# A re-planned prologue: first keys copied out of PSUM without their bias, two left-over values on four column quarters, left-over keys and values behind the second head's queries

## The chip, the cores and the metric

The kernel runs on one core of a Trainium2 chip. Its time is the device time of one execution in microseconds (us), as a median of several executions. Work is spread over five engines with queues of their own: PE (TensorE) multiplies and writes into PSUM, DVE (VectorE) and ACT (ScalarE) read PSUM and SBUF, POOL (GpSimd) works in SBUF, and SP issues most of the transfers between HBM and SBUF. An engine works through its queue in order and waits at an instruction until the semaphores it names are there.

## The reference

```
x   = residual + mha(layernorm(x), layernorm(ctx))      # 4096 queries, 3202 keys, H=512, 8 heads of 64
U   = (layernorm(x) @ W_in.T + b_in) @ Bmat
s_t = silu(s_{t-1} @ A.T) + u_t                          # 64 states, over the 4096 rows
out = x + states @ Cmat + (mean(ctxb) @ W_prog.T + b_prog)
```

Here only the front of it matters: keys `k = ln(ctx) @ Wk.T + bk` and values `v = ln(ctx) @ Wv.T` of all 3202 rows (the bias of the values goes into the output's row), and the queries of the first 512 rows. Everything is float32.

## The kernel before, in words

**Stages.** A prologue (`lead`) makes all keys and values and writes them to HBM (`kd`, `vd`), prepares weights, and makes the first queries. Then the main part goes over 8 blocks of 512 queries and 4 pairs of heads, loading keys and values again as it goes; each step is a pair of score and output products. The last part ends the recurrence. Only the prologue's order differs between the two kernels.

**The prologue.** The 3202 rows are 26 chunks: 25 of 128 rows and one of 2 (`REST`). Four chunks make a group; `ct` holds a group's normalized rows turned (features on the partitions), two groups at a time. Groups 0 and 1 are turned on PE (`tp_c`) and copied out of PSUM by ACT or DVE (`copy_chunk`); groups 2 to 5 are flipped by DVE in blocks of 32 (`pair`, L639) and moved into place by sixteen transfers on SP (`ct<-pair`, L651). The transfers of a group are numbered by four parts `a`; the first two parts hold the group's first two chunks.

Keys and values of a group come from a seven-product scheme (`Seven`), names `"1"` to `"7"`, each product being four matmuls of 128x256 (`pkx`, `pky`, `pvx`, `pvy`: the k or v side, bank x or y). Sums of quarters of `ct` (`t`, by DVE, L950) and of the weights (`sk`, `sv`, by POOL, L923) are operands. Bank x takes products 1, 6, 7, 4 in turn, bank y 2, 5, 3. After product 1 alone, `keep` copies bank x out of PSUM (outcome `"11"`); only then may product 6 go on adding into that bank. On the keys' side `keep` is two activations that add the key bias on the way; that bias (`wk.bias`) needs a chain of its own: four DVE instructions of `shift_wk`, four thin PE matmuls (`pb`, L1024) and a DVE sum (L1031). `join` (pieces `tied`) then adds bank y to the kept tile by DVE; product 5 may go into bank y only after that. `keep` for the other outcomes (`"12"`, `"22"`, `"21"`) works the same way.

Chunks 0 to 3 make values by plain products (`whole_chunk`, `pv`, four matmuls of 128x512). So does the end of the prologue: chunk 24 and the two rows of chunk 25. For those two rows `whole_chunk` splits the four matmuls over two column halves of the array (`parts = 2`), and `last_values` adds the two halves, which lie on different partitions of PSUM, and sends them to `vx`. `keys_` makes the keys of the 130 rows left (`pk`, L884), a copy to `ks`, and a POOL copy of the last two keys to `kx` (`k.sample`). `heads` makes queries of a head pair half (`pq`, L398), and ACT copies them out as `q` (L408). The first scores against a sample of keys are `sm` (L436): they read `q` of the first two and `kx` of the first two.

**What sets the order.** `Plan.order` is a list scheduler that runs while the program is built: each piece has a cost, pieces it comes after, rings of buffers it takes and gives, and a due time; the due time is shifted by the table `SHIFT`, in units of `STEP` (2150). The earliest due piece that fits is taken. The result is one fixed order for each queue; nothing of the plan's own times is left at run time, only the order and the semaphores.

Of the kernel before, what the change touches and what calls it, by code (L numbers as in the profile page):

```python
# [14 lines left out]
ALU = mybir.AluOpType  # L15
# [4 lines left out]
T, S2, H, NH, HD, NS = 4096, 3202, 512, 8, 64, 64  # L20
P = 128
# [55 lines left out]
class Plan:  # L77
# [18 lines left out]
    SHIFT = {  # L96
        "a": 1.5, "add": 0.5, "add.h": 776.5, "add.l": -24.5, "added": 171.75, "b": 1, "base": 34.5, "c2": -4,
# [20 lines left out]
        "swap.h": 43.75, "swap.l": -4, "to": -50, "tq": 14.75, "weights": -83.5, "yb": 20.5, "a.load": -109.5,  # L118
        "bu": -32.25, "c.copy": 24, "c.factors": -82.75, "c.flip": -34.5, "c.load": -5.25, "c.move": -90,
        "c.scaled": 21.25, "c.stats": 504.75, "c.turn": -1, "d.bi": 113, "d.bm": -0.75, "d.cb": 32,  # L120
        "d.cb2": -19.25, "d.rows": 117.75, "d.win": 69.25, "d.wo": 105.5, "d.wq": 96.5, "d.x0": 34.75,
        "h0": 166, "h0.q": 30, "in": 539.5, "in.bi": 32, "in.bm": 6.75, "in.cb": 28.25, "in.cb2": -22.5,
        "in.rows": 190.25, "in.win": -29, "in.wk": 608.5, "in.wo": 72.5, "in.wq": -22.25, "in.x0": 10.5,
        "k": 57, "k.copy": -98, "k.sample": -40.75, "k.store": 39.75, "keep": -66.75, "marks": -168.25,
        "mean": -21.5, "modb": -40.75, "p": -663, "pb": 39.25, "pm": -330, "prm": -87.25, "prr": 28.25,
        "pt": -27.5, "pw": -174.25, "rowb": -43, "rowv": -84, "rowv.w": 39.75, "s": -19, "store": -169.25,
        "sums_": -3.25, "t": -142, "tied": -298.5, "v": 1.5, "v.copy": -50.25, "v.store": -78.25,
        "wcr": 33.75, "wct": -20.25, "wk": -206, "wk.bias": -112.5, "wk.g": -107.25, "wk.pb": -197.75,
        "wk.w": -368.5, "wq": -85, "wq.bias": -56.25, "wq.g": -303, "wq.pb": 70.5, "wq.w": -109.25,
        "wv": 73.75, "wv.bias": 25.25, "wv.pb": -1.75, "wv.w": -148.25, "x.copy": -459.25, "x.factors": 8.25,  # L130
        "x.scaled": -133.75, "x.stats": -7, "x.turn": -793.75, "xh": -113.25, "fold": 21,
# [122 lines left out]
def xattn_ssm_kernel(  # L254
# [451 lines left out]
    class Seven:  # L706
# [18 lines left out]

        def keep(self, k, half):
            tag = self.tag + "s"
            t = self.kept[k] = cin.tile([P, 2, QU], F32, tag=tag, name=f"{tag}_{self.g}_{k}")
            if not self.of_keys:
                nc.scalar.copy(t, self.x)  # L730
                return
            for b in range(2):
                hp = 2 * half + b
                nc.scalar.activation(  # L734
                    t[:, b], self.x[:, b], AF.Identity, bias=bias[:, NC + hp : NC + hp + 1]
                )

        def join(self, k):
            t = self.kept[k]
            nc.vector.tensor_tensor(t, self.y, t, ALU.add)  # L740
# [9 lines left out]
    def whole_chunk(c, pv):  # L750
        n = keys(c)
        ct, o = cts[c // GC], c % GC * CK
        parts = 1 if c < NCH - 1 else 2
        for i in range(NC // parts):
            for h in range(parts):
                k = h * NC // parts + i
                nc.tensor.matmul(  # L757
                    pv[h * HD : h * HD + n, :H],
                    ct[:, k, o : o + n],
                    wv[:, k, :],  # L760
                    start=(i == 0),
                    stop=(i == NC // parts - 1),
                    skip_group_check=True,
                )
# [12 lines left out]
    def lead():  # L777
# [77 lines left out]
        def values(c):  # L855
# [13 lines left out]
            add(("v", c), "PE", 3560 if c < NCH - 1 else 1800, product, there(c), u, ["v"], [ct_of(c // GC)])  # L869
# [61 lines left out]
        def group(g, lefts):  # L931
# [36 lines left out]
            for at_, (a, k) in enumerate(  # L968
# [15 lines left out]
                if k in outs:  # L984
                    c, half, pair = outs[k]
                    gives = [(tag, ("p", g, a, "1"))] if k == "4" else []
                    add(("keep", g, a, c), "ACT", 600 if a else 1000, partial(s.keep, c, half), [("p", g, a, k), "wk.bias"],
                        u + SLOT, [tag + "s"], gives)
                tie = {"2": ("11", 0, 0), "7": ("22", 1, 1), "3": ("12", 0, 1)}.get(k)
                if tie:  # L990
                    c, half, pair = tie
                    gives = [(tag, ("p", g, a, "2"))] if k == "3" else []
                    add(("tied", g, a, c), "DVE", 690, partial(s.join, c),
                        [("keep", g, a, c), ("p", g, a, "5" if k == "7" else k)], u + SLOT + 500, [], gives)
# [239 lines left out]
        for at_, (load, k) in enumerate(loads):  # L1234
# [1668 lines left out]
```

## Time and profile before

| | |
|---|---|
| median of 3 executions | 1871.13 us (1867.05 to 1872.38) |
| the profiled execution, its own time | 1869.18 us |
| its span, first to last instruction | 1867.4 us |
| mean granted TensorE clock | 0.998 |
| busy: PE, DVE, ACT, POOL | 99%, 80%, 61%, 14% |
| the first query scores of the main part (L1321) on PE | from 198.84 us of the span |

The profiled execution lies 1.78 us above its span and 1.95 us under the median. The prologue is about the first 199 us. In a row of the chain or the timeline the first column is the start in us from the span's begin, the second the length; the name is output<-inputs. In a row by stretches, each engine's busy us stand in turn, then the granted TensorE clock (1.00 is full), the DMA share and GB/s.

### The profile page before, as it was taken

To read this page: it belongs to the slowest core of one execution; us is meant where nothing else is said; L and a number is where in the kernel's file an instruction comes from. 1 tells how busy PE (TensorE), PEld (TensorE's weight loads), DVE (VectorE), ACT (ScalarE), POOL (GpSimd) and SP (SyncE) were. 2 spreads that over 40 slices of the span, in tenths; PEclk is the share of its full clock that TensorE was granted. 3 is DMA by queue.
4 is the path that set the end of the run, shared out by engine and by line. 5 is a ranking of instruction groups with operands and counts; after the bars stand their busy time and mean duration, and the time that the engine had idled before them with its cause. 6 is when DMAs were issued, how large, how long until landed. Compare 5 with 4: busy or idle time off the path is not lost.

```text
span 1867.4 us, 44587 instructions
## 1 busy us (share of the span) xinstructions
PE 1849.3 (99%) x17948; PEld 1048.2 (56%) x17948; DVE 1495.5 (80%) x1745; ACT 1139.9 (61%) x1409; POOL 262.1 (14%) x393
## 2 busy tenths in 40 slices
PE   9999999999999999999999999999999999999997
PEld 6887333433363456335643456466736674777674
DVE  7752688788878887888878887888888897889776
ACT  3342667577756774776656774677477665657653
POOL 4220301000210021000110021002010011120105
PEclk9999999999999999999999999999999999999999
DMA  7673142134214331434233421533143423646477
GB/s 234 184 203 106 60 122 72 40 100 139 66 37 141 90 92 43 116 97 134 55 94 103 139 67 36 142 84 92 49 113 95 140 55 88 171 121 183 142 204 229
DMA packets 262641, 209.01 MB, mean 112 GB/s; under 512 B 87502, under 2 KB 235870, under 8 KB 262432
## 3 DMA queue, kind: packets, MB, share of 16 engines
q1 hardware_dynamic: 258412, 199.50, 37.7%
q10 hardware_dynamic: 4020, 6.62, 1.2%
q8 instruction: 143, 2.34, 0.5%
q14 instruction: 66, 0.54, 0.1%
HBM read 157.24 MB, written 29.89 MB: 100 GB/s over the span
## 4 chain that ended last, share of the span: by engine, by line
PE 94%; DVE 3%; DMA 1%; ACT 1%; SPq 1%; issue 0%; POOL 0%; DVEq 0%; POOLq 0%; ACTq 0%
PE po L1427 31%; PE s L1321 31%; PE po L1452 4%; PE s L1334 4%; PE qx L543 3%; PE pax L543 3%; PE pay L543 2%; PE qy L543 2%; PE pkx L543 2%; PE pvx L543 1%; DVE acc L1373 1%; PE pky L543 1%; PE pvy L543 1%; PE pv L757 1%; PE pd L1481 1%; PE po L1416 1%
## 5 line engine op out<-in xcount | busy, mean ns | idle before, releaser
L1365 ACT ACTIVATE p<-s,shifts 128x1024 f32<-128x1024 f32 x804 | 886.9, 1109 | 400.6 <-PE s L1321 330.1
L1373 DVE TENSOR_TENSOR acc<-p,acc 128x1024 f32<-128x1024 f32 (+1 forms) x732 | 899.2, 1230 | 91.6 <-ACT p L1365 59.5
L1321 PE MATMUL s<-q,k 64*64 64x512 f32 x5600 | 755.8, 589 | 0.3 <-ACT p L1365 0.3
L1427 PE MATMUL po<-p,v 64*64 64x512 f32 x5600 | 755.9, 589 | 0.0
L1321 PEld LDWEIGHTS s<-q,k 64*64 64x64 f32 x5600 | 269.7, 133 | 324.8 <-issue 267.6
L1427 PEld LDWEIGHTS po<-p,v 64*64 64x64 f32 x5600 | 270.8, 133 | 306.1 <-issue 267.2
L1609 POOL TENSOR_SCALAR rstd_x<-mv_x 128x1 f32<-128x1 f32 x28 | 14.7, 525 | 827.8 <-DVE mv_x L1606 559.0
L1539 DVE RECIPROCAL rd<-rd 128x256 f32<-128x256 f32 (+1 forms) x64 | 109.8, 1718 | 1.2 <-ACT rd L1534 1.0
L1334 PE MATMUL s<-q,k 64*64 64x256 f32 x1600 | 109.4, 377 | 0.5 <-ACT p L1365 0.5
L1452 PE MATMUL po<-p,v 64*64 64x256 f32 x1600 | 109.8, 377 | 0.0
L1934 POOL TENSOR_TENSOR xr<-x,modb 128x512 f32<-128x512 f32 x28 | 36.4, 1310 | 364.0 <-DVE x L1884 292.0
L1334 PEld LDWEIGHTS s<-q,k 64*64 64x64 f32 x1600 | 67.5, 133 | 24.4 <-issue 4.0
L1452 PEld LDWEIGHTS po<-p,v 64*64 64x64 f32 x1600 | 68.7, 133 | 17.3 <-issue 1.2
L1373 DVE TENSOR_TENSOR acc<-p,p 128x1024 f32<-128x1024 f32 x36 | 44.0, 1223 | 32.2 <-ACT p L1365 31.8
L1834 POOL TENSOR_TENSOR xr<-xr,rowb 128x512 f32<-128x512 f32 x28 | 47.3, 1709 | 102.4 <-DMA xr<-in_x_dram 53.7
L456 ACT COPY ex<-sm 128x512 f32<-128x512 f32 (+1 forms) x18 | 8.8, 542 | 75.0 <-PE sm L436 75.0
L1350 DVE SCALAR_TENSOR_TENSOR swap<-ex,marks,swap 128x512 f32<-128x512 f32 (+1 forms) x35 | 24.8, 709 | 35.4 <-ACT swap L1396 35.1
L734 ACT ACTIVATE ks<-pkx,bias 128x256 f32<-128x256 f32 x48 | 20.1, 469 | 49.6 <-PE pkx L543 46.3
L1396 ACT COPY swap<-acc 64x512 f32<-64x512 f32 (+1 forms) x70 | 40.2, 574 | 16.4 <-DVE acc L1380 12.2
L1760 ACT ACTIVATE q<-qx,bias 128x256 f32<-128x256 f32 x42 | 17.6, 470 | 45.3 <-PE qx L543 45.3
L1401 DVE TENSOR_TENSOR acc<-swap,acc 64x512 f32<-64x512 f32 (+1 forms) x70 | 44.1, 631 | 1.1
L1515 DVE TENSOR_TENSOR o<-po,o 128x512 f32<-128x512 f32 (+1 forms) x36 | 22.7, 631 | 24.5 <-ACT o L1508 24.0
(307 smaller groups left out, 1730.3 us busy)
## 6 DMA issues: line engine op xcount, KB each, us to landing
k<-kd SPq DMA_DIRECT2D x432, 128.0 KB, 2.6
v<-vd SPq DMA_DIRECT2D x432, 128.0 KB, 2.6
xn<-x SPq DMA_DIRECT2D x448, 32.0 KB, 1.9
xr<-in_x_dram SPq DMA_DIRECT2D x30, 256.0 KB, 4.8
x1d<-xr SPq DMA_DIRECT2D x30, 256.0 KB, 2.8
x<-in_x_dram SPq DMA_DIRECT2D x28, 256.0 KB, 3.9
cx<-in_ctx_dram SPq DMA_DIRECT2D x25, 256.0 KB, 3.2
kd<-ks SPq DMA_DIRECT2D x24, 256.0 KB, 2.3
```

What stands on the lines that cost most here:

```text
L543: nc.tensor.matmul(to[:, b, :], still[:, i, b * P : (b + 1) * P], moving[:, i, :], start=(start and b == 0 and i == 0), stop=(i == 1), ski ...
L1321: nc.tensor.matmul(s[k0 : k0 + HD, a].rearrange("p b j -> p (b j)"), kts[(*w["at"][:2], c // 2)][r, b * CK + k0 : b * CK + k0 + HD], q[r], ...
L1334: nc.tensor.matmul(s[k0 : k0 + HD, a, b, :], kts[(*w["at"][:2], c)][r, b * CK + k0 : b * CK + k0 + HD], q[r], start=True, stop=True, skip_ ...
L1365: nc.scalar.activation(t[:, :, :nb, :], w["ps"][c][:, :, :nb, :], AF.Exp, bias=w["shift"])
L1373: return nc.vector.tensor_tensor(w["acc"][:, :, :nb, :], t[:, :, :nb, :], before[:, :, :nb, :], ALU.add)
L1396: nc.scalar.copy(w["swap"][r], of[(1 - k) * HD : (2 - k) * HD])
L1401: made = nc.vector.tensor_tensor(of[r], w["swap"][r], of[r], ALU.add)
L1427: nc.tensor.matmul(w["po"][k][a * HD : (a + 1) * HD], vts[Q, hp, c // 2][r, c % 2, a * HD : (a + 1) * HD], t[r, a].rearrange("p b j -> p ( ...
L1452: nc.tensor.matmul(w["po"][k][a * HD : (a + 1) * HD, :QU], vts[Q, hp, c][r, b, a * HD : (a + 1) * HD], t[r, a, b, :], start=(c == 0 and b ...
L1539: nc.vector.reciprocal(w["rd"][:, part], (w["pd"] if last else w["rd"])[:, part])
L1834: return nc.gpsimd.tensor_tensor(xs[half][:, t], xs[half][:, t], rowb, ALU.add)
L1934: return nc.gpsimd.tensor_tensor(xt[:, t], x1[:, t], modb, ALU.add)
```

## The change

1. The first keys (group 0, outcome `"11"`) leave PSUM by one plain ACT copy, without bias, and so without waiting for it (`bare`). The bias is added in `join`, by two DVE instructions of 128x256 in place of one of 128x512. `join` now waits for the bias.
2. The two rows of chunk 25: the four matmuls go to four column quarters (`parts = NC`), and `last_values` adds four pieces, with three DVE sums in place of one.
3. The table `SHIFT` for the prologue's pieces is new, so the order of the prologue changes on every queue: among others the left-over keys and values (`pv`, `pk` of chunks 24 and 25) now stand behind the second head's queries. A piece `lead.end` is added that issues nothing. Entries of the main part stay, and its order is as before.

```diff
+        def bare(self, k):
+            return self.of_keys and self.g == 0 and k == "11"
         def keep(self, k, half):
...
-            if not self.of_keys:
+            if not self.of_keys or self.bare(k):
                 nc.scalar.copy(t, self.x)
                 return
...
         def join(self, k):
             t = self.kept[k]
+            if self.bare(k):
+                for b in range(2):
+                    nc.vector.scalar_tensor_tensor(
+                        t[:, b], self.y[:, b], bias[:, NC + b : NC + b + 1], t[:, b], ALU.add, ALU.add
+                    )
+                return
             nc.vector.tensor_tensor(t, self.y, t, ALU.add)
...
-        parts = 1 if c < NCH - 1 else 2
+        parts = 1 if c < NCH - 1 else NC
...
-                    pv[h * HD : h * HD + n, :H],
+                    pv[h * P // parts : h * P // parts + n, :H],
...
-        nc.scalar.copy(second, pv[HD : HD + n])
-        nc.vector.tensor_tensor(second, pv[:n], second, ALU.add)
+        nc.scalar.copy(second, pv[:n])
+        for r in range(P // NC, P, P // NC):
+            nc.vector.tensor_tensor(second, pv[r : r + n], second, ALU.add)
...
-                    add(("keep", g, a, c), "ACT", 600 if a else 1000, partial(s.keep, c, half), [("p", g, a, k), "wk.bias"],
+                    add(("keep", g, a, c), "ACT", 600 if a or bare else 1000, partial(s.keep, c, half),
+                        [("p", g, a, k)] + ["wk.bias"][bare:], u + SLOT, [tag + "s"], gives)
...
-        "swap.h": 43.75, "swap.l": -4, "to": -50, "tq": 14.75, "weights": -83.5, "yb": 20.5, "a.load": -109.5,
+        "a.load": 20, "c.copy": 10.25, "c.factors": 3, "c.flip": 20.25, "c.load": -30.25, "c.move": -12,
...
+        after = [("h0.q", hp) for hp in range(FIRST)] + [("k.sample", n_g, hp) for hp in range(2)]
+        add("lead.end", "PE", 2500, lambda: None, after, 1e6)
```

PE around the second product into bank x of group 0's keys, before (`pv` are values, `tp_c` turns a chunk, the first `pkx` is product 1, the second is product 6):

```order
L757 MATMUL pv_331<-wv,ct_188 128x512 x4
L368 MATMUL tp_c_363<-ident,xh_c_288 128x128 x4
L368 MATMUL tp_c_371<-ident,xh_c_320 128x128 x4
L543 MATMUL pkx_382<-ct_188,wk 128x256 x4
L543 MATMUL pky_395<-ct_188,wk 128x256 x4
L543 MATMUL pvx_407<-wv,ct_362 128x256 x4
L543 MATMUL pvy_422<-wv,ct_362 128x256 x4
L1024 MATMUL pb_433<-ones,shift_wk 128x1 x4
L368 MATMUL tp_c_441<-ident,xh_c_324 128x128 x4
L368 MATMUL tp_c_449<-ident,xh_c_378 128x128 x4
L543 MATMUL pkx_382<-t_0_322,sk_427 128x256 x4
```

and now:

```order
L367 MATMUL tp_c_339<-ident,xh_c_288 128x128 x4
L367 MATMUL tp_c_348<-ident,xh_c_314 128x128 x4
L765 MATMUL pv_357<-wv,ct_188 128x512 x4
L367 MATMUL tp_c_380<-ident,xh_c_330 128x128 x4
L542 MATMUL pkx_387<-ct_188,wk 128x256 x4
L542 MATMUL pky_400<-ct_188,wk 128x256 x4
L542 MATMUL pvx_414<-wv,ct_338 128x256 x4
L542 MATMUL pvy_420<-wv,ct_338 128x256 x4
L367 MATMUL tp_c_436<-ident,xh_c_353 128x128 x4
L1036 MATMUL pb_443<-ones,shift_wk 128x1 x4
L542 MATMUL pkx_387<-t_0_344,sk_398 128x256 x4
```

Three of the four turns of group 1 stand ahead of product 1 now, and the bias's thin product stands last ahead of product 6.

DVE in the same place, before (L623 scales the key weight, L633 and L1031 end the bias, L740 is `join`, L950 makes sums of `ct`):

```order
L950 TENSOR_TENSOR t_0_336<-ct_188,t_0_322 128x512
L331 BN_STATS st_c_343<-cx_232 128x6
L333 BN_AGGR mv_c_345<-st_c_343 128x2
L623 TENSOR_SCALAR wk<-raw_k,g1s 128x512 x4
L688 COPY ct_362<-tp_c_371 128x4x128
L630 TENSOR_SCALAR shift_wk<-raw_k,be1s 128x512
L633 SCALAR_TENSOR_TENSOR shift_wk<-raw_k,be1s,shift_wk 128x512 x3
L623 TENSOR_SCALAR wq<-raw_q,g1s 128x512 x4
L1031 TENSOR_TENSOR bias<-pb_433,bqkv 128x4
```

and now:

```order
L687 COPY ct_338<-tp_c_348 128x4x128
L622 TENSOR_SCALAR wk<-raw_k,g1s 128x512 x4
L330 BN_STATS st_c_376<-cx_280 128x6
L332 BN_AGGR mv_c_378<-st_c_376 128x2
L330 BN_STATS st_c_394<-cx_306 128x6
L332 BN_AGGR mv_c_396<-st_c_394 128x2
L629 TENSOR_SCALAR shift_wk<-raw_k,be1s 128x512
L632 SCALAR_TENSOR_TENSOR shift_wk<-raw_k,be1s,shift_wk 128x512 x3
L687 COPY ct_338<-tp_c_436 128x4x128
L1043 TENSOR_TENSOR bias<-pb_443,bqkv 128x4
L744 SCALAR_TENSOR_TENSOR ks_11_409<-pky_400,bias,ks_11_409 128x256 x2
L748 TENSOR_TENSOR vs_11_456<-pvy_420,vs_11_456 128x512
```

The statistics of two more chunks stand ahead of the bias's chain, the scaling of the query weight (`wq`) has gone behind it, and the new two-part join stands right behind the bias.

PE at the prologue's end, before (`pq` are queries, the second `pv` is chunk 25):

```order
L398 MATMUL pq_0_1511<-xn_1126,wq 128x512 x4
L757 MATMUL pv_1517<-wv,ct_1495 128x512 x4
L757 MATMUL pv_1524<-wv,ct_1495 2x512 x4
L884 MATMUL pk_0_1532<-ct_1495,wk 128x130 x4
L884 MATMUL pk_1_1544<-ct_1495,wk 128x130 x4
L884 MATMUL pk_2_1553<-ct_1495,wk 128x130 x4
L884 MATMUL pk_3_1562<-ct_1495,wk 128x130 x4
L398 MATMUL pq_1_1571<-xn_1126,wq 128x512 x4
L436 MATMUL sm_0_0_1619<-q_0_1522,kx 32x256
```

and now:

```order
L397 MATMUL pq_0_1493<-xn_1255,wq 128x512 x4
L367 MATMUL tp_c_1502<-ident,xh_c_1128 128x128 x4
L367 MATMUL tp_c_1509<-ident,xh_c_1142 128x2 x4
L1164 MATMUL prr<-shift_rowv,ones 128x512
L397 MATMUL pq_1_1518<-xn_1255,wq 128x512 x4
L765 MATMUL pv_1524<-wv,ct_1501 128x512 x4
L765 MATMUL pv_1530<-wv,ct_1501 2x512 x4
L893 MATMUL pk_0_1538<-ct_1501,wk 128x130 x4
L893 MATMUL pk_1_1552<-ct_1501,wk 128x130 x4
L893 MATMUL pk_2_1561<-ct_1501,wk 128x130 x4
L893 MATMUL pk_3_1570<-ct_1501,wk 128x130 x4
L435 MATMUL sm_0_0_1621<-q_0_1507,kx 32x256
```

Between the second queries and the sample's scores that read them stand now six products, where none stood. On SP, the sixteen `ct<-pair` transfers of group 2 stood as 8, 4 and 4 with nine stores in between; now they stand as 12 and 4 with four stores in between.

More of the change, by code (lines that the diff above doesn't have):

```diff
@@ L117 @@
         "stored0": -101, "stored1": -91.75, "sums": 40, "sums.h": 11.5, "sums.l": -285.75, "swap": 4,
-        "swap.h": 43.75, "swap.l": -4, "to": -50, "tq": 14.75, "weights": -83.5, "yb": 20.5, "a.load": -109.5,
[L119 to L131, printed above, removed]
+        "swap.h": 43.75, "swap.l": -4, "to": -50, "tq": 14.75, "weights": -83.5, "yb": 20.5, "fold": 21,
     }
@@ L867, in store @@
                 nc.sync.dma_start(vd[:, c // 2, :, c % 2, :].rearrange("h p d -> p h d"), v["vs"])
-            add(("v", c), "PE", 3560 if c < NCH - 1 else 1800, product, there(c), u, ["v"], [ct_of(c // GC)])
+            add(("v", c), "PE", 3560 if c < NCH - 1 else 900, product, there(c), u, ["v"], [ct_of(c // GC)])
             if c == NCH - 1:
@@ L992, in group @@
                     gives = [(tag, ("p", g, a, "2"))] if k == "3" else []
-                    add(("tied", g, a, c), "DVE", 690, partial(s.join, c),
-                        [("keep", g, a, c), ("p", g, a, "5" if k == "7" else k)], u + SLOT + 500, [], gives)
+                    bare = s.bare(c)
+                    add(("tied", g, a, c), "DVE", 850 if bare else 690, partial(s.join, c),
+                        [("keep", g, a, c), ("p", g, a, "5" if k == "7" else k)] + ["wk.bias"][: bare],
+                        u + SLOT + 500, [], gives)
                 if k in "2743":
```

13 lines of the change are left out of this document (12 added, 1 removed).

## The prediction

> **What bounds the kernel now.** I read the page's busy lines and its chain first, then the stretches, then the waits of PE in the prologue, then the chain in order of time at each of those waits.
>
> ```profile
> span 1867.4 us, 44587 instructions
> PE 1849.3 (99%) x17948; PEld 1048.2 (56%) x17948; DVE 1495.5 (80%) x1745; ACT 1139.9 (61%) x1409; POOL 262.1 (14%) x393
> PE 94%; DVE 3%; DMA 1%; ACT 1%; SPq 1%; issue 0%; POOL 0%; DVEq 0%; POOLq 0%; ACTq 0%
> ```
>
> PE is the bound, and 94% of the chain that ended last is its work. So a change to the order can win only what PE lost by waiting or by a low clock, and a change to PE's own work wins what it takes out. Stretches show how much there is (length, PE, PEld, DVE, ACT, POOL, granted clock, DMA share, GB/s):
>
> ```profile
> 0.00:60.00 60.00, 57.11 (x244) 42.60 (x245) 48.82 (x87) 21.39 (x38) 28.07 (x63) 0.97 0.70 219
> 60.00:200.00 140.00, 138.85 (x658) 110.49 (x660) 56.45 (x112) 46.70 (x89) 23.59 (x59) 1.00 0.57 158
> 200.00:600.00 400.00, 399.99 (x3684) 163.27 (x3680) 329.71 (x337) 268.20 (x296) 43.01 (x48) 1.00 0.30 83
> ```
>
> PE idles 2.89 us in the first 60 us and 1.15 us in the next 140; in the first 400 us of the main part it idles 0.01. The first 60 us also have a clock of 0.97. The waits of PE up to 230 us name the places (us in total, times, longest):
>
> ```profile
> PE pkx L543 <- ACT ks L734: 1.1, 1, 1.1
> PE sm L436 <- ACT q L408: 0.9, 1, 0.9
> PE pv L757 <- ACT ct L688: 0.5, 1, 0.5
> PE pvy L543 <- DVE t L950: 0.3, 1, 0.3
> ```
>
> The third (`pv`) is the second product of the kernel and lies ahead of everything that the change touches. The other three are the places to look at; the rest of the idling is PE's start.
>
> **Part 1, the first keys without bias.** The chain in order of time (start, length):
>
> ```profile
> 16.83 6.87 PE pv L757 x16
> ...
> 31.48 0.79 PE pb L1024 x8
> 32.27 0.51 PE tp_c L368 x4
> 32.80 0.05 ACT ct L688
> ...
> 33.28 0.85 ACT ks L734 x2
> ...
> 34.27 3.53 PE pkx L543 x8
> 37.80 1.85 PE pky L543 x8
> 39.65 1.73 PE pkx L543 x8
> ```
>
> Product 6 (`pkx` at 34.27) waited for the two activations with bias, which stood behind a copy of `ct`, while the bank they read had been filled ahead of `pb`. PE idled 1.07 us. And product 6 then took 3.53 us where its like takes 1.73: the clock was halved, as the stretches show.
>
> ```profile
> 35.00:36.00 1.00, 1.00 (x4) 0.79 (x3) 1.00 (x2) 0.55 (x1) 1.00 (x2) 0.50 0.36 137
> 38.00:39.00 1.00, 1.00 (x6) 0.90 (x5) 0.98 (x2) 0.68 (x2) 0.04 (x1) 1.00 0.66 194
> ```
>
> That is 3.53 + 1.85 - 2 x 1.73 = 1.92 us more. Now the copy out of PSUM stands right behind product 1, with three products and more between it and product 6, and even at the 0.85 us of the two activations it is over by then. So 1.07 + 1.92 = 2.99 us are to be had, if nothing else is late at product 6 and the clock then stays up.
>
> What is late next is the bias itself, since its thin product `pb` now stands directly ahead of product 6. The rows for its DVE chain and for POOL beside it:
>
> ```profile
> 21.36 1.65 DVE L623 TENSOR_SCALAR wk<-raw_k,g1s 128x512 f32<-128x512 f32 x4
> 25.22 1.48 DVE L630 TENSOR_SCALAR shift_wk<-raw_k,be1s 128x512 f32<-128x512 f32 x1
> 26.73 4.10 DVE L633 SCALAR_TENSOR_TENSOR shift_wk<-raw_k,be1s,shift_wk 128x512 f32<-128x512 f32 x3
> 42.95 0.74 DVE L633 SCALAR_TENSOR_TENSOR shift_wq<-raw_q,be1s,shift_wq 128x512 f32<-128x512 f32 x1
> 20.47 0.69 DVE L331 BATCH_NORM_STATS2 st_c<-cx 128x6 f32<-128x512 f32 x1
> 20.47 0.26 POOL L344 TENSOR_SCALAR nmr_c<-mv_c,rstd_c 128x1 f32<-128x1 f32 x1
> 25.14 1.27 POOL L923 TENSOR_TENSOR sk<-wk 128x512 f32<-128x512 f32 x1
> ```
>
> Four turns instead of two stand ahead of `pb` (0.45 to 0.5 us each, by the 0.51), so PE comes to it at 31.48 + 0.9 = 32.4. DVE's four scalings of the weight now stand behind a copy of the second of two turns that follow the first of the two `pv` products: 16.83 + 6.87 / 2 + 0.9 and some 0.7 for the copy (a reading of 128x512 like the statistics' 0.69), 21.9. Alone they take 1.65 and end at 23.5. With POOL's sums beside them, each DVE instruction takes as long as a POOL sum (1.48 against a quarter of 1.65). But POOL can put only its three value sums there, 3 x 1.27 = 3.8 us from the end of its factors at 20.73, and its next one needs the scaled weight: the scalings end by about 25.2. Product 1 needs two of the four at about 25.0, product 2 the others 1.73 later, so that costs nothing. Two chunks' statistics (0.69, with the rest of each about 0.9) end by 27.1. The chain of `shift_wk` takes 4 x 0.74 = 3.0 us alone and 1.48 + 4.10 = 5.6 beside POOL, and ends between 30.1 and 32.7. Against 32.4 that is a stall of 0 to 0.3 us; I take 0.1.
>
> [...]
>
> The join now is two instructions of 128x256 with three operands; no row shows that form. One of 128x512 took 0.74, so it lies between 0.74 and 1.48; near the lower end, since half the elements are in each: 0.9. Product 5 may start after it. The bias is there about 0.2 after product 6 starts, the join ends about 1.2 after, product 6 takes 1.73: hidden, with the 1.48 too. Behind the join on DVE, one more join and a sum of `ct` must be ready for product 7, and POOL's next sum may block the latter: 0 to 0.3 us, I take 0.2. The activations left out of ACT's queue cost nothing there.
>
> **Part 2, group 2.** PE waited 0.28 us at 79.20 for a DVE sum that waited for the moved group:
>
> ```profile
> 68.30 6.86 DMA ct<-pair
> ...
> 78.45 0.70 DVE t L950
> ...
> 79.20 1.99 PE pvy L543 x8
> 71.78 4.62 SPq L651 DMA_DIRECT2D ct<-pair  x4
> 68.03 0.38 ACTq L1078 DMA_DIRECT2D wo<-in_L_xattn_W_o_dram  x1
> ```
>
> These transfers went beside the load of `wo` and took up to 6.86 us. Now twelve of sixteen are issued in one go, and the last four stand behind the store of outcome `"21"` of group 1. From that product's end to group 2's product 6, PE has six products of 1.73 and three thin ones of some 0.8 (as `pb` at 31.48), some 13 us. On the other side stand the two activations (0.85), the store's issue (as one of four in 4.62, 1.2), four issues (4.62), a landing (6.86) and two sums (0.70 each): 14.9 us if every one is as bad as the worst seen before. So the 0.28 us go, unless nearly all bad values meet again, which would cost up to 1.9. I take a gain of 0.28, since the issues now find twelve of the sixteen already done. Nothing in the trace waits at groups 3 to 5, and their order keeps its distances.
>
> **Part 3, the end of the prologue.**
>
> ```profile
> 177.44 5.25 PE pv L757 x16
> 182.69 3.77 PE pk L884 x32
> 186.46 3.45 PE pq L398 x8
> 189.93 0.70 ACT q L408
> ...
> 190.76 0.79 PE sm L436 x16
> ...
> 200.71 0.59 PE sm L436 x16
> 185.60 0.37 ACT L894 ACTIVATE ks<-pk,bias 128x130 f32<-128x130 f32 x1 [0.53 <-PE pk L884]
> 186.03 0.18 POOL L904 COPY kx<-ks 128x2 f32<-128x2 f32 x1 [0.71 <-ACT ks L894]
> ```
>
> The copy of the second queries (0.70 and its signals, 0.87 of idle PE) had no cover: `sm` stood right behind. Now two `pv` and four `pk`, some 8 us, stand in between, and cover it. `sm` also needs `kx` of the first two heads: those copies (0.37 + 0.18 and signals) have the third and fourth `pk` (3.77 / 4 = 0.94 each) ahead of `sm`. So 0.87 us go. In the next step DVE's three sums of two rows and the seven stores come later against the main part, by the 3.45 us of `pq`; the first exponentials come some 9 us behind `sm`, so they do not meet.
>
> The two rows of chunk 25 took 5.25 - 6.87 / 2 = 1.82 us: four matmuls in two rounds. On four quarters they take one round, 0.91, if all four run at once. `sm` speaks for it: its eight matmuls on quarters and halves took 0.59 for sixteen records, far less than one after another. Ends: 0 and 0.91 gained; I take 0.91. The sums after it (two more on DVE) hide behind four `pk`.
>
> **The sum.** 2.99 + 0.28 + 0.87 + 0.91 = 5.05 us, less 0.3 for the two small stalls: 4.75 us. The profiled execution goes from 1869.18 to 1864.4. The median lay 1.95 above it, and I carry that over: 1871.13 - 4.75 = 1866.4 us. No more than the 5.05 and the 0.5 at the first `pv` can be won at all, 5.5 us, since the main part has no idle PE and its order stays. 0.3%, about what a measurement of this kernel can tell from no change, is 5.6 us.
>
> **The rivals.**
> - *The bias is the new wait.* POOL gets in ahead of every DVE instruction: scalings of 4 x 1.48 = 5.9 us to 27.8, statistics to 29.6, the chain of 5.6 to 35.2. PE then waits 2.8 us at `pb`, more than the 1.07 of before, and the clock falls (1.92): of the 5.05 us some 0.3 are left, 1870.8. Against it: POOL has only three sums to put there.
> - *The clock halves again at product 6.* The stretch before the fall held thin work too (`pb`, two turns) beside 1.07 us of idling; against that, PE idled 0.87 us at 190, and the stretch from 60 to 200 kept a clock of 1.00. If the thin stretch is enough, 1.92 us stay: gain 2.8, 1868.3. Against it also: the idling is gone or a fourth of what it was.
>   [...]
> - *Group 2 is late.* All the bad values: 1.9 us, and perhaps another fall of the clock (1.92): gain 0.7 to 2.6, 1869.5.
> - *The quarters run in two rounds.* Gain 3.8: 1867.3.
> - *Slower than before.* The last four transfers of group 2 behind one more store or beside `wo` and the four row loads: PE waits from 13 us after outcome `"21"` on, one for one. From 17.8 us on, all the gain is gone; the worst sum of seen values is 14.9. With a landing of twice 6.86 it would be 21.8: 4.0 us slower, and a fall of the clock 1.9 more, 1877.
> - *It does nothing*, that is, the plan moves the waits elsewhere in the 60 to 190 us where PE is full now, by as much: 1871.
>
> **How the numbers follow.** Forecast 0.61; bias 0.04; clock 0.11; group 2 0.09; quarters 0.05; nothing 0.05; slower 0.05. The forecast's own range is 1864 to 1869 by its ends and the three runs' spread of 5.3 us. The range 1862 to 1871 takes in the clock, group 2 and quarters. Faster by over 0.3% needs nearly all of the 5.5 us or the help of scatter: about half of the forecast's chance, 0.29. Slower by over 0.3% is the slower case, 0.05. Within: 0.66.
>
> **What would show it.** Right: `pkx` of product 6 near 33.2 with 1.7 us, clock 1.00 in every us from 30 to 40; no wait of `pvy` or `pkx` for `t` near 77; the second `pv` at the end 0.9 us; `sm` directly behind `pk`; first scores at about 194. Wrong: a wait of `pb` for `shift_wk` over 0.5 us, a stretch of clock 0.50, a wait named `ct<-pair`, or `sm` waiting for POOL's `kx`.

## The result, and the profile after

Timed side by side, the changed kernel took 1864.13 us in the median of 7 executions (1862.04 to 1865.33) and the kernel before 1869.37 us (1866.29 to 1872.38): a ratio of 0.9972, 95% interval 0.996 to 0.9983. That is 5.2 us or 0.28% less, and 2.3 us under the forecast of 1866.4, most of it because the kernel before itself came out 1.8 us lower than in its first three executions. The profiled execution of the changed kernel took 1865.33 us, with a span of 1863.5. Its page:

```profile
span 1863.5 us, 44582 instructions
...
PE 96%; DVE 1%; DMA 1%; issue 0%; ACT 0%; SPq 0%; POOL 0%; DVEq 0%; POOLq 0%; ACTq 0%
```

By stretches (length, PE, PEld, DVE, ACT, POOL, clock, DMA share, GB/s):

```profile
0.00:60.00 60.00, 57.56 (x262) 43.76 (x263) 48.82 (x92) 21.05 (x38) 29.75 (x63) 1.00 0.75 237
60.00:200.00 140.00, 139.33 (x692) 108.70 (x690) 59.69 (x113) 51.95 (x95) 24.44 (x59) 1.00 0.55 153
35.00:36.00 1.00, 1.00 (x7) 0.82 (x5) 1.00 (x1) 0.47 (x2) 0.91 (x2) 1.00 1.05 395
```

PE is still the bound. Its idling went from 2.89 to 2.44 us in the first 60 us and from 1.15 to 0.67 in the next 140, and the clock is full near product 6. PE's waits up to 226 us show which went and which came (L542 was L543, L765 was L757):

```profile
PE pkx L542 <- DMA ct<-pair: 0.7, 1, 0.7
...
```

The waits of product 6, of `sm` for `q` and of `pvy` for `t` are gone. A new one of 0.7 us is at the *first* product of group 2. (Besides PE's start, the rows left out are ahead of everything that the change touches: 0.5 us at the second `pv`, as before, and two of 0.4 us at the first turns, which vary between profiles of both kernels, 0.6 and 0.4 in the second profile of before and none in its first.) In order of time, at product 6 and at the end of the prologue:

```profile
31.98 0.79 PE pb L1036 x8
32.76 1.83 PE pkx L542 x8
34.60 1.73 PE pky L542 x8
...
168.99 3.43 PE pq L397 x8
...
177.68 4.41 PE pv L765 x16
182.08 3.77 PE pk L893 x32
185.85 1.12 PE sm L435 x16
...
194.26 1.88 PE s L1335 x16
```

Product 6 starts 1.51 us earlier and takes 1.83 us; the two `pv` take 4.41 us instead of 5.25; `sm` follows `pk` at once, but takes 1.12 us instead of 0.79. The first scores come at 194.26 instead of 198.84.

### The profile page after: what moved, and what is told of

The parts are those of the page before. It is cut to its first block, busy times and chain, and to the rows that moved or that the text cites. A ratio compares the mean times of both kernels' runs of the same rounds, so it can differ in the third digit from the quotient of the medians.

```text
span 1863.5 us, 44582 instructions
## 1 busy us (share of the span) xinstructions
PE 1847.1 (99%) x17948; PEld 1027.5 (55%) x17948; DVE 1496.5 (80%) x1748; ACT 1141.1 (61%) x1408; POOL 265.1 (14%) x393
## 3 DMA queue, kind: packets, MB, share of 16 engines
q8 instruction: 143, 2.34, 0.6%
## 4 chain that ended last, share of the span: by engine, by line
PE 96%; DVE 1%; DMA 1%; issue 0%; ACT 0%; SPq 0%; POOL 0%; DVEq 0%; POOLq 0%; ACTq 0%
PE po L1441 32%; PE s L1335 32%; PE po L1466 5%; PE s L1348 4%; PE qx L542 3%; PE pax L542 3%; PE pay L542 2%; PE qy L542 2%; PE pkx L542 2%; PE pvx L542 2%; PE pky L542 1%; PE pvy L542 1%; PE pv L765 1%; PE pd L1495 1%; PE pu L1966 1%; PE po L1430 1%
## 5 line engine op out<-in xcount | busy, mean ns | idle before, releaser
L1441 PE MATMUL po<-p,v 64*64 64x512 f32 x5600 | 747.4, 589 | 0.0
L1335 PE MATMUL s<-q,k 64*64 64x512 f32 x5600 | 747.3, 589 | 0.0
L1335 PEld LDWEIGHTS s<-q,k 64*64 64x64 f32 x5600 | 259.6, 133 | 334.2 <-issue 289.4
L1441 PEld LDWEIGHTS po<-p,v 64*64 64x64 f32 x5600 | 261.1, 133 | 315.2 <-issue 288.3
L1348 PEld LDWEIGHTS s<-q,k 64*64 64x64 f32 x1600 | 67.7, 133 | 24.6 <-issue 4.0
L1466 PEld LDWEIGHTS po<-p,v 64*64 64x64 f32 x1600 | 69.2, 133 | 17.4 <-issue 1.2
```

What stands on the lines that cost most here:

```text
L1335: nc.tensor.matmul(s[k0 : k0 + HD, a].rearrange("p b j -> p (b j)"), kts[(*w["at"][:2], c // 2)][r, b * CK + k0 : b * CK + k0 + HD], q[r], ...
L1348: nc.tensor.matmul(s[k0 : k0 + HD, a, b, :], kts[(*w["at"][:2], c)][r, b * CK + k0 : b * CK + k0 + HD], q[r], start=True, stop=True, skip_ ...
L1441: nc.tensor.matmul(w["po"][k][a * HD : (a + 1) * HD], vts[Q, hp, c // 2][r, c % 2, a * HD : (a + 1) * HD], t[r, a].rearrange("p b j -> p ( ...
L1466: nc.tensor.matmul(w["po"][k][a * HD : (a + 1) * HD, :QU], vts[Q, hp, c][r, b, a * HD : (a + 1) * HD], t[r, a, b, :], start=(c == 0 and b ...
```

## The experiments

Three questions were left: what dropped the clock at product 6, what each part is worth by itself, and what the new wait of group 2 is. The chain gives the start of the first scores (`s`) in each profile, so places can be compared far below the spread of whole executions.

**The clock at product 6: idling or thin work?** First, undoing `bare` in the changed kernel:

```diff
         def bare(self, k):
-            return self.of_keys and self.g == 0 and k == "11"
+            return False
```

> The changed kernel with the first keys taken out of PSUM with the bias again (two activations that wait for the bias, then one sum as the join); order near product 6 and quarters stay as changed. Theory 1 (the copy without bias removed the idling ahead of product 6, and idling of about 1 us is what drops the clock): the bias is ready some 0.3 us behind pb, the two activations take 0.85, so PE idles 1.1 to 2.0 us ahead of product 6 and the clock shows 0.50 there; product 6 and the next take 5.3 to 5.4 us instead of 3.5; first scores at 197.3 to 198.2 instead of 194.26. Rival (the new order alone, with two turns fewer around pb, removed both): no idle above 0.3 us, product 6 at 1.7 to 1.8 us, first scores at 194.3 to 194.8.

Its wait and chain at product 6, and the stretches there:

```profile
PE pkx L542 <- ACT ks L736: 1.2, 1, 1.2
```
```profile
32.86 0.17 DVE bias L1043
...
33.43 0.47 ACT ks L736
34.04 1.97 PE pkx L542 x8
36.01 1.73 PE pky L542 x8
```
```profile
30.42:33.83 3.41, 2.41 (x18) 2.14 (x16) 2.87 (x5) 0.77 (x3) 0.66 (x1) 1.00 0.29 53
33.83:37.24 3.41, 3.20 (x15) 2.87 (x16) 3.41 (x6) 1.38 (x4) 2.18 (x4) 1.00 0.82 294
```

The idling is back, 1.2 us, more than the 1.07 of before: the wait was that of the bias, and the copy without bias is what took it away. But product 6 runs at full clock (1.00 from 33.83 to 37.24). So here 1.2 us of idling did not drop it by itself, and that half of theory 1 falls. (The first scores come at 199.45: with this wait come others, of 1.1 and 0.8 us, and one spell, that is a stretch at half clock, from 67.97 to 71.38.)

Then the opposite, thin work without idling, eight thin matmuls ahead of product 6 in the changed kernel:

```diff
+                    if g == 0 and k == "6":
+                        thin = m_tile([P, 512], "thin")
+                        for j in range(8):
+                            nc.tensor.matmul(thin[:, j : j + 1], wk[:, 0, :P], ones[:, 0:1], start=True, stop=True)
                     s.product(k)
```

> The changed kernel with eight more thin matmuls (128x1, the form of pb) directly ahead of product 6, whose results nobody reads. Theory 1 (idling drops the clock, thin work does not): product 6 starts about 1.6 us later (eight such at 0.2 us), PE stays without an idle time above 0.2 us there, product 6 and the next take 1.7 to 1.8 us each and the clock shows 1.00 from 30 to 40; first scores at 195.8 to 196.0. Rival (a long stretch of thin work, here some 2.8 us, is enough): a stretch of 0.50, product 6 and the next take about 5.4 us together, first scores at 197.7.

```profile
31.35:34.77 3.42, 3.42 (x31) 3.32 (x31) 2.78 (x7) 0.58 (x1) 0.44 (x2) 1.00 0.49 128
34.77:38.18 3.41, 3.41 (x10) 2.69 (x10) 3.41 (x6) 0.00 (x0) 2.94 (x4) 0.50 0.96 329
```

PE is busy for 100% of the 3.42 us ahead, and the clock halves all the same (0.50 from 34.77 to 38.18). Here thin work was enough. The slip of 2 us has a price of its own: ACT's copy of later keys comes behind loads in its queue (ACT is idle for 10.47 us before it starts at 64.95), PE waits 4.6 us at about 62 us, and the first scores come at 203.2, much later than either theory said.

Third, the kernel before with its gap filled:

```diff
+                    if s.of_keys and s.g == 0 and k == "6":
+                        nc.tensor.matmul(m_tile([P, 512], "fill"), wk[:, 0, :P], wk[:, 0, :], start=True, stop=True)
                     s.product(k)
```

> The kernel before with one matmul of 128x512, whose result nobody reads, directly ahead of product 6, in the 1.07 us in which PE idled. Theory 1 (the idling dropped the clock): the dummy takes about 0.87 us, the rest of the idling is 0.2 us, product 6 still starts near 34.3, but at full clock: 1.73 us, and the next 1.73; first scores 1.8 to 1.9 us earlier than the 198.84 of before, 197.0. Rival (the thin work ahead, pb and two turns, dropped it): the dummy itself or product 6 run at half clock, a stretch of 0.50 is there, first scores at 198.5 to 199.7.

```profile
33.91 1.97 PE pkx L543 x8
35.88 1.73 PE pky L543 x8
```
```profile
73.85:77.26 3.41, 3.25 (x18) 2.02 (x16) 1.50 (x4) 0.84 (x2) 0.00 (x0) 1.00 0.77 221
77.26:80.67 3.41, 3.28 (x8) 2.65 (x9) 3.34 (x8) 0.00 (x0) 0.00 (x0) 0.50 0.56 110
```

Product 6 is at full clock, as theory 1 had it, but the first scores come at 198.63 and not at 197.0: a spell of half clock now stands at 77.26, behind the thin products `pm`, `pb`, `prm` of group 2. And since the kernel before without the filling also runs product 6 at full clock in two of its three profiles (below), this run alone does not show that the filling did it.

**A grid.** Each spell in these traces that ends before the kernel does is 3.41 us long. And in each trace all spells start on one grid of 3.4133 us (starts read from stretches of 0.05 us): 34.51 and 1864.05 in the trace before (536 steps apart), 67.97 and 1832.66 in the first experiment (517 steps), 77.26 and 1831.71 in the third (514). The grid's offset differs from execution to execution: counted back in such steps, its first points lie at 0.38, 3.12 and 2.17 us of these three spans. From this came theory 2, the author's reading: the clock is judged in windows on this grid, and a window with too little heavy work is followed by one at half clock. The traces show the length and the grid; that the work in a window decides, and what counts as heavy, is assumed. PE's busy share by itself did not decide: the window from 31.35 to 34.77 in the second experiment, with PE busy for 100%, was followed by one at 0.50. Theory 2 was tested on the unchanged kernel before:

> The kernel before, unchanged, for a second profile. Theory 2 (the clock is judged in windows of 3.41 us that run on freely; a window with too little heavy work is followed by one window at half clock; heavy work is matmuls of 256 columns and more, thin work and idling count alike): the stretch from 31.48 to 34.27 is low, so product 6 runs at half clock only if a window's edge falls near the end of it, surely for an edge between 34.3 and 34.9 and perhaps between 33.7 and 35.5 (0.63 us of heavy work was followed by a fall, 1.18 us was not); 18 to 52 in 100 runs. If the edge, read back in steps of 3.413 us from the spell at the kernel's end, lies elsewhere, product 6 takes 1.7 to 2.0 us and the first scores come at 196.9 to 197.3; all spells of the run start on one grid. Theory 1 (about 1 us of idling there drops the clock each time) and the rival that thin work does: 0.50 again, 3.53 us, first scores at 198.8.

```profile
PE pkx L543 <- ACT ks L734: 1.1, 1, 1.1
```
```profile
31.59:35.00 3.41, 2.34 (x16) 2.03 (x16) 3.13 (x9) 2.42 (x5) 1.55 (x5) 1.00 0.88 295
35.00:38.42 3.42, 3.42 (x17) 3.01 (x17) 3.38 (x4) 1.03 (x3) 2.65 (x2) 1.00 0.51 168
```
```profile
33.87 1.97 PE pkx L543 x8
...
196.86 1.88 PE s L1321 x16
```

The same kernel, the same wait, and no fall; first scores 1.98 us earlier than in its first profile. Read back from the spell at this execution's end, its windows' edges lie at 31.59 and 35.00, so the window with the gap also holds 1.13 us of product 6. In the first profile the edges were at 31.09 and 34.51, with 0.39 us of `pvy` and 0.24 of product 6 inside, 0.63 in all, although PE was busy just as long:

```profile
31.09:34.51 3.42, 2.35 (x19) 2.10 (x18) 3.11 (x9) 1.71 (x4) 0.86 (x3) 1.00 0.70 216
34.51:37.92 3.41, 3.41 (x9) 2.72 (x9) 3.38 (x4) 0.98 (x3) 3.20 (x4) 0.50 0.56 189
```

> The kernel before, unchanged, for a third profile. Theory 2: all spells of half clock start on one grid of 3.413 us. In this kernel's own times the low stretch goes from the end of pvy to the start of product 6; if a window holds no more than 0.63 us of heavy work beside the stretch, product 6 runs at half clock (3.5 us and first scores about 25.0 us after the second pq's start as always, but 2.0 us later from product 1 on); if it holds 1.13 us or more, product 6 takes 1.73 to 1.97 us; between these nothing is known yet. Chance of a fall by the bounds so far: 18 to 48 in 100. Theory 1: a fall, always.

No fall at product 6 (1.97 us after 1.1 us of idling; its window, 30.16 to 33.58, held 1.0 us of `pvy`), but one at 77.95, again behind group 2's thin products, and the first scores at 198.65:

```profile
74.54:77.95 3.41, 3.17 (x18) 2.21 (x18) 2.23 (x6) 0.34 (x1) 0.00 (x0) 1.00 0.69 182
77.95:81.36 3.41, 3.41 (x10) 2.71 (x9) 3.34 (x8) 0.00 (x0) 0.00 (x0) 0.50 0.44 86
```

Count as heavy the matmuls of products and values, up to where the next piece of the chain starts, and as not heavy the turns, `pb`, `pm`, `prm` and idling. Then windows with 0.38 (thin matmuls), 0.63, 0.63 and 0.65 us of heavy work were followed by a fall, and windows with 0.8 to 0.9 (the first profile, 75.47 to 78.88), 1.0, 1.13 and 1.18 us (the first experiment) were not. Matmuls overlap in the trace (the records of one 128x256 product stretch over 1.89 us, and the next product starts 1.73 us after it), so other ways of counting move these figures by up to 0.2 us; the two groups stay apart. PE's busy share does not sort them: falls after 100%, 95%, 93% and 69%, none after 69% (2.34 of 3.41) and 71%. But one window does not fit: 64.55 to 67.97 in the first experiment held some 1.3 us and was followed by a fall. Weighing turns and `prm` at about half makes all nine fit by one way of counting and not by another, so what the hardware counts stays open. Shown are the grid of 3.4133 us, the length of 3.41, a fall behind a window with PE busy for 100%, and the same stretch at 0.50 in one execution and at 1.00 in two others.

**The parts by themselves.** Chunk 25 on halves again, in the changed kernel:

```diff
-        parts = 1 if c < NCH - 1 else NC
+        parts = 1 if c < NCH - 1 else 2
...
```

> The changed kernel with chunk 25's two rows on two column halves again (two rounds of two matmuls, one sum behind them). Theory 1 (four column quarters run at once): the two pv products take 5.25 us together instead of 4.41, first scores at 195.1 instead of 194.26. Rival (the gain at this place was of the clock or of the place, not of the quarters): pv stays at 4.4, first scores at 194.3.

```profile
176.97 5.25 PE pv L765 x16
...
194.40 1.88 PE s L1334 x16
```

`pv` takes 5.25 us: the quarters are worth 0.84 us. The first scores come only 0.14 later than in the changed kernel, because group 2's wait for `ct<-pair` was absent in this execution, though the order there is the same.

The second pair's queries behind the left-over keys again:

```diff
-                [("x.copy", t) for t in range(NT)] + ["wq", "wq.bias"] + ([("h0.q", hp - 1)] if hp % 2 else []), d,
+                [("x.copy", t) for t in range(NT)] + ["wq", "wq.bias"] + ([("h0.q", hp - 1)] + [("k", n_g, x) for x in range(NC)] if hp % 2 else []), d,
```

> The changed kernel with the second pair's queries behind the left-over keys again, directly ahead of sm. Theory (the move covered the copy of the queries): sm waits 0.85 to 0.9 us for q, sm itself takes 0.79 us since the bank's copy is long over; from the start of the first pq to the first scores 25.27 + 0.87 - 0.33 = 25.8 us. Rival (the wait only changes place, so the move brought nothing): 25.2 to 25.4. The rest is the changed kernel a third time.

```profile
169.78 3.43 PE pq L397 x8
...
183.21 3.45 PE pq L397 x8
...
186.69 0.70 ACT q L407
...
187.52 0.65 PE sm L435 x12
...
195.46 1.88 PE s L1335 x16
```

From the first `pq` to the first scores it is 25.68 us against 25.27. The wait for the queries' copy is back (`pq` ends at 186.66, `sm` goes on at 187.52; four of its records ran ahead of the wait), but the move is worth 0.41 us only, since `sm` itself is shorter here. Why, the next one shows, with `sm`'s matmuls sorted by PSUM tile:

```diff
-                        for a in range(2):
+            order_ = [(a, i) for a in range(2) for i in range(4)] if not Q and not gs[0] else [
+                (a, i) for i in range(4) for a in range(2)
+            ]
...
```

> The changed kernel with the eight matmuls of sm in another order: the four of its first PSUM tile, then the four of its second, instead of in turn. Theory (the second tile takes the PSUM bank of the last left-over keys, so sm's second matmul waits for ACT's copy of these at 186.26 and all others queue behind it): the first four run in that wait, sm takes about 0.8 us instead of 1.12, and from the start of the first pq to the first scores it is 24.95 us instead of 25.27. Rival (sm as a whole waits for the copies, or its matmuls only run at once in the old order): 25.27 or more. Up to sm it is the changed kernel a second time: by theory 2 the spells of half clock lie on a grid with another phase, none in the first 200 us; the wait for ct<-pair of 0.67 us comes again if it is of the plan, not if it is of the transfers' chance.

```profile
186.01 0.15 PEld L437 LDWEIGHTS sm<-q,kx 64*32 64x32 f32 x8
186.12 0.37 ACT L905 ACTIVATE ks<-pk,bias 128x130 f32<-128x130 f32 x1 [0.52 <-PE pk L895]
186.54 0.15 PEld L437 LDWEIGHTS sm<-q,kx 64*32 64x32 f32 x8 [0.38 <-ACT ks L905]
```
```profile
186.08 1.10 PE sm L437 x16
```

The first tile's eight loads run through and the second's eight wait for the copy of the last keys: the second tile does stand on that copy's PSUM bank. But `sm` takes 1.10 us all the same: the second tile's loads start at 186.54, and from there its half alone takes another 0.63 us, where all of `sm` took 0.79 before. Why a half by itself is so slow was not tested. The wait is as the theory has it, the remedy is not; the rival was right on the time.

The new code with the old table of due times:

> The changed kernel's code with the old table of numbers that sets the order: pb, two turns and then product 6 as before, and the second queries behind the left-over keys. Theory (the copy without bias does part 1 by itself): no idling above 0.2 us ahead of product 6, which starts at 33.2 to 33.4 and takes 1.7 to 2.0 us whatever the grid's phase, since the low stretch is only some 1.8 us; chunk 25 takes 0.9 us; sm still waits 0.87 us for q; first scores at 194.7 to 195.2 if group 2 is on time. Rival (the new order is needed for it): product 6 waits, for another release, 0.5 us or more.

```profile
PE pkx L543 <- ACT ks L737: 3.7, 2, 2.7
PE pky L543 <- DVE t L960: 1.8, 1, 1.8
...
```
```profile
64.15 1.13 ACTq L1088 DMA_DIRECT2D a_t<-in_L_xattn_A_dram  x2
65.38 0.58 ACT L733 COPY vs<-pvx 128x512 f32<-128x512 f32 x1 [5.96 <-DMA cx<-in_ctx_dram]
```

Product 6 is on time (32.87, 1.73 us), the two `pv` take 4.40 and `sm` waits 0.9 us, as expected. But the first scores come at 208.6, ten us *later* than before, and the execution took 1878.74 us beside 1868.32 for the kernel before. With the bias out of the copy, the old table gives another order: the next `pkx` stands directly behind product 6. A wait of 1.0 us comes there, later ACT stands 6 us behind a load in its queue, PE waits 2.7 us for a copy of keys behind it and 1.8 for a sum, and the clock stays at half from 67.5 to 84.5. Neither theory had this: the code makes the gain possible, the new table keeps it.

**Group 2's new wait.** Two ways to clear the transfers' path, each holding back loads on ACT's queue:

```diff
-        fetched("wo", ..., 6000, [("p", 1, 0, "4")], 45000)
+        fetched("wo", ..., 6000, [("p", 1, 0, "4")] + [("c.move", FLIPS * GC, a) for a in range(4)], 45000)
```

> The changed kernel with the 1 MB load of wo held back until the sixteen transfers of group 2 are issued (the order of a few later pieces shifts with it). Theory (the wait of group 2's first product for ct<-pair, 0.67, 0.4 and 0.5 us in three profiles of this order and none in a fourth, comes from the last of the first twelve transfers, which land in 5.18 us because wo moves beside them): the wait is gone, these transfers land in 2 to 3.5 us, and the first scores come 0.4 to 0.7 us earlier, at 193.6 to 194.0; the time is lower by as much, less than these rounds tell (0.03%): 0.996 to 0.999 of the kernel before. Rival (the transfers are slow because they queue behind older stores and loads on SP): the wait stays at 0.4 to 0.7 us. Second rival: wo comes too late for something, and PE waits elsewhere before 226 us.

> The changed kernel with the small row loads of ACT's queue (rowb, modb and two more, in all about 0.6 MB, issued from 50.3 to 56.5 us) held back behind group 2's transfers instead. Theory (wo is what delays the last transfers, since the rows have landed by then): the wait for ct<-pair stays at 0.4 to 0.7 us, or is absent as in one of four profiles. Rival (the rows make the whole chain of transfers start and land late: SP's first transfer waits 1.9 us for a store beside them): the first of the twelve is issued before 54.2 instead of 54.77, the last before 64.0, and the wait is gone. For both: ACT's queue, which stood 5.7 us at these loads, is free, and its copies of keys come earlier without a gain.

 (The edit is the same, at `rows`.)

The wait is gone in both profiles, which by itself says little, since it was also absent in one of the five without these edits. The landings say more: the slowest of these sixteen transfers lands in 2.1 us with `wo` held back and in 2.7 with the rows held back, against 5.0 to 5.7 us in the five. Holding back either traffic was enough, in one profile each. (The median does not tell them apart: it is 2.2 us in two of the five too.) The first scores come later in both. The first, waits and chain:

```profile
PE pvx L542 <- ACT vs L732: 1.0, 1, 1.0
PE pkx L542 <- ACT ks L736: 0.9, 1, 0.9
```
```profile
196.23 1.88 PE s L1335 x16
```

The second, on ACT and on PE:

```profile
77.08 0.84 ACT L736 ACTIVATE ks<-pkx,bias 128x256 f32<-128x256 f32 x2 [6.04 <-DMA wp_t<-in_L_xattn_W_prog_dram]
```
```profile
77.97 3.78 PE L542 MATMUL pkx<-t,sk 128*128 128x256 f32 x8 [4.58 <-ACT ks L736]
```

ACT's queue stood at the loads in both places, 5.7 us in the changed kernel and 6.0 here; in the changed kernel PE needed no copy from ACT just then, and it cost PE nothing. Held back, they hit group 2's keys: 4.58 us of idling, two windows at half clock (76.62 to 83.45), first scores at 201.16. With `wo` held back the median of 12 was 1866.35 us, but four of them took 1870.28 to 1873.24, and the ratio is 0.9996 (0.9987 to 1.0006): not shown to be better than the kernel before, and worse than the changed one (0.9972). So neither keeps the gain and loses the wait.

Last, the changed kernel once more:

> The changed kernel, unchanged, timed in five rounds for the spread of its time. Theory 2 (what the change takes away is the low stretch ahead of product 6 and with it one place where a window can fall, besides about 2.5 us of waiting and work): all runs between 1861.5 and 1866.5 with the median at 1863.5 to 1865, the kernel before between 1865 and 1873, ratio 0.9965 to 0.9985; the profile has no spell of half clock in the first 200 us, and the first scores between 193.6 and 194.9. Rival (the places where a slip of one us turns into a stall of four, as the held-back loads showed, are met by the changed kernel too in some executions): a second group of runs some 5 us above the first, and a ratio near 0.999.

Median 1864.72 us of 10 (1862.76 to 1866.31), the kernel before 1869.68 of 14 (1866.4 to 1871.27), ratio 0.9975 (0.9965 to 0.9984): as expected, and no second group. That does not tell theory 2 from a fixed price of the idling; the three profiles of before do. The first scores came later than the 193.6 to 194.9 expected, behind a wait that the other profiles of this order did not have:

```profile
PE pvx L542 <- ACT vs L732: 0.8, 1, 0.8
PE pkx L542 <- DMA ct<-pair: 0.3, 1, 0.3
```
```profile
195.32 1.88 PE s L1335 x16
```

## Why the prediction was right, and where it was not

**The gap at product 6** (1.07 us): right, for the reason given; 1.2 us come back with the bias. The bias was no new wait: `shift_wk` ended at 31.59 (forecast 30.1 to 32.7) and PE came to `pb` at 31.98, straight from a turn. Beside POOL's value sums DVE's four scalings took 3.93 us and ended at 25.33 (forecast 25.2); the first rival had 5.9 us. The join took 0.88 us for both instructions (forecast 0.9). Neither small stall came, so the 0.3 us set off for them were not lost there.

**The clock** (1.92 us): this step was sized wrongly. The prediction took the fall as a fixed cost of the idling. It is a fall by chance: the kernel before idled 1.1 us in all three of its profiles and lost the clock there in one. By theory 2, a low stretch of 2.79 us lies wholly within one window for 0.62 us of the 3.41 us of offsets, and with a bound of 0.65 to 0.9 us of heavy work (by the windows of this kernel) up to 0.27 us on each side come to it: an estimate of 20 to 34 falls in 100 executions, with the window that does not fit left aside. What the prediction did not see is the second such place, group 2's thin products and the wait behind them, some 2.8 us. Of the four profiles with the order of before (its three, and the one with the filled gap), three have a spell in the first 200 us, one at product 6 and two at group 2; of the five with the changed order that ran as planned there (the changed kernel twice, the halves, `sm`, the queries), none. The longest low stretches there are 1.22 us at product 6 and 1.9 at group 2. With the same chance at both places that is 0.4 to 0.7 spells of some 1.7 us less (3.53 + 1.85 against 1.97 + 1.73), about 1 us in the mean, an estimate that rests on four profiles and on that bound.

**Group 2** (0.28 us): the wait named was removed, but the sum looked at product 6 only. The first half of the same transfers is needed by the first product, 9 us earlier, and there PE waited 0.67, 0.4, 0.5, 0.3 and 0 us in five profiles. A wait named `ct<-pair` was listed as a sign of being wrong, and it is one.

**The queries** (0.87 us): 0.41 by the experiment. The wait is covered, but `sm` now stands right behind the last left-over keys, and half of it waits for ACT to clear their PSUM bank: 1.12 us against 0.79. The prediction had checked `kx` and `q`, the inputs, and not the output's bank.

**The quarters** (0.91 us): 0.84. The two `pv` took 4.41 us on quarters and 5.25 on halves, near what one round in place of two was to give.

**The sum.** Take the second profile of before, which has no spell in the prologue, and count from the span's start. Product 6 ends at 34.60 us instead of 35.84, a gain of 1.24. (From product 1's start it looks like more, 9.97 us instead of 11.67, but 0.44 of that is a turn that now stands ahead of product 1.) From there to `sm` it is 151.25 us instead of 152.95, a gain of 1.70 (0.87 and 0.84 are 1.71, so all else between cancels). `sm` to the first scores loses 0.34. That is 2.60 us, and the first scores come at 194.26 instead of 196.86; the changed kernel's other profile, with them at 195.32, has 1.54. With about 1 us of spells it makes 2.5 to 3.6. The forecast's 4.75 was 2.83 of steady gain, near the 2.60, and 1.92 of clock in each execution, about twice what the runs give it in the mean.

Measured were 5.2 and 5.0 us between medians, more than the parts found. All executions whose clock is on record, sorted by it (a spell of 3.41 us at half is 0.0009 of the span):

| clock | before: median, executions | changed: median, executions |
|---|---|---|
| 1.000, 0.999 | 1867.5 us, 7 | 1863.9 us, 6 |
| 0.998 | 1869.0 us, 9 | 1864.1 us, 3 |
| 0.997 | 1868.8 us, 4 | 1864.6 us, 7 |
| 0.996, 0.995 | 1870.3 us, 15 | 1865.5 us, 1 |

At equal clock some 3.6 to 4.9 us separate them, and the kernel before has more executions with a low clock. The steady gain of the traces explains 1.5 to 2.6 us of the first. The rest, 1.0 to 3.4 us, is not placed. It is not behind the first scores: from there to the span's end it is 1668.6 us on average in three profiles of before and in five of the changed order alike, between 1667.7 and 1669.5. And the executions that were profiled show less of it: 1868.6 us in the mean of three of before and 1865.3 of two of the changed kernel, 3.3 us apart. So that the forecast came within 0.5 us of the measured gain is in part luck: a clock term that was too large stands where some us of gain are not explained.

Of the rivals, the bias was no wait, and the quarters brought 0.84 us; the transfers of group 2 were late by part of the worst sum; the clock rival was right that thin work can be enough to drop the clock (0.50 behind the eight thin matmuls), but the thin stretch that is left at product 6 (1.22 us) did not drop it in any profile of the planned order.

## What to carry to other kernels

In three profiles of the kernel before, the same idling of 1.1 us at product 6 was followed by a low clock once. So read a low clock in one trace as one draw: find the grid from two spells, and ask in how many executions a stretch of thin work and waiting of that length would be caught. As far as these runs tell, stretches of 1.2 to 1.9 us stayed free of spells in five profiles; heavy work between thin products was tried once (the filled gap), without a clear answer. And where a fixed order is tuned as a whole, a better piece of code alone can make it worse, here by ten us in the one execution with the old table: search the order anew with the code.

## What the runs showed of the hardware that was not expected

- Half-clock spells (0.50) of 3.41 us, or of two (6.83, with the rows held back) and five (17.07, with the old table) such windows, on one grid of 3.4133 us through a whole execution, and PE busy for 100% of the window ahead of one (31.35 to 34.77, the thin matmuls).
- 1.2 us of idling behind thin work left the clock at 1.00 in one execution (window edges at 30.42 and 33.83), while 1.07 us in another were followed by 3.41 us at half clock (edges at 31.09 and 34.51).
- Loads in ACT's queue held it for 3.8 us (the first experiment), 5.7 (the changed kernel), 6.0 (the rows held back) and 10.5 (the thin matmuls). After a slip of 2 us at product 6 (thin matmuls), or with the loads issued 20 us later (rows held back), PE waited 4.6 us for a copy of keys that stood behind them: at about 62 us and at 77.97.
